# A two-layer graph network on one core: projections by seven half-size products, and layer 1's ELU spread over more steps

## The chip, the cores and the metric

The kernel runs on one core of one Trainium2 chip. Its time is the device time of one execution in microseconds (us), and the median of the runs counts. The engines are TensorE (PE), VectorE (DVE), ScalarE (ACT), GpSimd (POOL) and SyncE (SP, which issues most DMAs). Each runs its own instructions in the order in which the program lists them, and waits on semaphores for the others. Everything of weight is in float32; only the masks and the small logit products of layer 1 are bfloat16.

## The reference

There are 4096 nodes with 512 features, and a 4096 x 4096 weighted adjacency matrix `adj`. Each of the two layers normalizes its input, applies relu, runs an attention and adds the result to its input.

```python
h = relu(layernorm(x))                       # layer 0
q, k, v = h @ Wq.T + bq, h @ Wk.T + bk, h @ Wv.T + bv
x = x + softmax(q @ k.T / sqrt(512) + 2 * adj) @ v
h = relu(layernorm(x))                       # layer 1: 8 heads of 64
nX = a_ln * standardized(h @ W, per head) + b_ln
kg = leaky_relu(at1[:, None] + at2[None, :], 0.2) * adj      # per head
y = softmax(where(adj != 0, kg, -32768)) @ nX + nX
x = x + elu(y)
```

## The kernel before

**Projections** (in `fast_path`, lines 545 to 701). The 4096 rows are taken in 8 blocks of 512. `normalize` (L558) takes means and variances of a block (bn_stats, L180), an inverse root (L167 to L172, the power on POOL) and scales the rows on DVE (L564). `hidden` (L569) transposes the block on PE, applies relu on ACT (L575) into `hT`, and forms four sums of quarter blocks, `hS`, on POOL (L583 to L586), both of which are stored for attention. `values_of` (L591) makes 4 tiles of v, each with four matmuls of 512 columns (L595) and one addition of the bias on DVE (L599). `queries` (L604) makes 4 tiles of q against the matrix A, which is Wq and Wk multiplied ahead (L669), in the same way (L609, L613), and forms four sums on POOL (L626 to L629). Four PSUM tiles (tag mm) hold results. The order is that of the program: in round sb it is `normalize` of block sb + 1, `load_x` of block sb + 2, `values_of(sb)`, `hidden(sb + 1)`, the small work on layer 1's weights (`center_weights` L236, `weigh_weights` L242), `queries(sb)`. Ahead of the rounds stands a prologue: loads of x, Wv, Wq and Wk, `turn_blocks` of Wq and Wk on DVE (L485), `values_of(0)`, `attention_vectors` (L200), A, `hidden(1)` and `queries(0)`.

**Attention of layer 0** runs over 8 chunks of 512 rows and 32 tiles of columns. Its scores are made by seven half-size products in place of eight (L740): a 2 x 2 block product in Winograd's form of Strassen's scheme, with sums of the operands formed ahead and results added on DVE (L748). The change does not touch it.

**Layer 1** runs 512 steps: 8 chunks of 512 rows, 2 groups of 4 heads, 32 column tiles. In step n the program issues `values(n - 4)` (PE, L1025), `exponent(n - 3)` (ACT, L1012, 2048 elements), `leaky(n)` (DVE: two operations L996, one product with adj L1001, one addition L1002), `weigh(n)` (POOL, L1009: the product with adj), `z_sums(n + 1)` (PE, L970 and L978, into three PSUM tiles with tag d) and `relu(n + 1)` (ACT, L986). POOL multiplies three heads and DVE one; in a "light" step DVE multiplies two and POOL two. Light are steps 11, 17, 23 and 29 of every 32 (L909). `load_adj` (L912) loads masks (z, nb, nx) and weights (g) for four steps at a time on SP.

When the 32 steps of a group are over, `finish` (L1030) hangs its work on the steps that follow, through a table of offsets d. "mid" is behind the exponent on ACT, "end" behind relu. It copies the sums out of PSUM (L1041), turns them into rows (`to_rows`, PE, L1047), divides (`divide`, DVE, L1056 and L1057), adds own features with a DMA that accumulates (`add`, issued on POOL, L1063), computes ELU in pieces on ACT (`minus` L1072, `exps` L1076, `positive` L1079, `less_one` L1082), adds the two halves and the residual with two more such DMAs, and stores (`close`, SP, L1087). As step n of the table is the fourth step of the next group, offset d falls into step d + 3 of that group.

Of the kernel before, what the change touches and what calls it, by code (L numbers as in the profile page):

```python
# [78 lines left out]
def fast_path(  # L79
# [161 lines left out]

    def weigh_weights(k):  # L242
        for e in range(2):
            t = prep.tile([P, NH, HD], F32, name="prod", tag="prod", bufs=2)
            seq(nc.gpsimd.tensor_mul(t, w1_sb[:, k], aa[e]))
            seq(nc.vector.tensor_reduce(w1a_sb[:, k, e, :], t, AX.X, ALU.add))
# [221 lines left out]
    with tc.tile_pool(name="early", bufs=2) as early, tc.tile_pool(name="kv", bufs=1) as kv:  # L468
# [70 lines left out]
        with tc.tile_pool(name="proj_c", bufs=1) as pc, tc.tile_pool(  # L539
# [10 lines left out]
            bv_sb = early.tile([P, D], F32, name="bv_sb", tag="qt", bufs=16)  # L550
# [7 lines left out]
            def normalize(xt):  # L558
                mv = means(work, [xt[:, b, :] for b in range(SB)], "h")
                var = work.tile([P, SB], F32, name="hv", tag="hv", bufs=1)  # L560
                seq(nc.vector.tensor_scalar_add(var, mv[:, :, 1], LN_EPS))
                rstd = inverse_root(nc.vector, work, var, SB, "h")
                for b in range(SB):
                    seq(nc.vector.tensor_scalar(  # L564
                        xt[:, b, :], xt[:, b, :], mv[:, b, 0:1], rstd[:, b : b + 1],
                        ALU.subtract, ALU.mult,
                    ))
# [22 lines left out]

            def values_of(sb):  # L591
                for b in range(SB):
                    pv = psum.tile([P, 512], F32, name="pv", tag="mm", bufs=4)
                    for k in range(KC):
                        seq(nc.tensor.matmul(  # L595
                            pv, hidden_of[sb][0][:, k, ts(b, P)], wv_sb[k],
                            start=k == 0, stop=k == KC - 1,
                        ))
                    seq(nc.vector.tensor_add(v[:, sb * SB + b, :], pv, bv_sb))  # L599
# [3 lines left out]

            def queries(sb):  # L604
                qs = pc.tile([P, KC, GC], F32, name="qs", tag="qs", bufs=1)
                for o in range(KC):
                    pq = psum.tile([P, 512], F32, name="pq", tag="mm", bufs=4)
                    for k in range(KC):
                        seq(nc.tensor.matmul(  # L609
                            pq, a_sb[:, k, ts(o, P)], hidden_of[sb][0][:, k, :],  # L610
                            start=k == 0, stop=k == KC - 1,
                        ))
                    seq(nc.vector.tensor_scalar(  # L613
                        sources_of_rows(qs[:, o, :]), pq.rearrange("p (c q r) -> p c q r", c=SB, r=R),
                        c_sb[:, o : o + 1], half_scale, ALU.add, ALU.mult,
                    ))
# [36 lines left out]
            normalize(xts[0])  # L653
# [3 lines left out]
            for name in ("q", "k"):  # L657
                for c in range(SB):
                    turn_blocks(turned[name][:, c, :], raw[name], c)
            values_of(0)  # L660
            normalize(xts[1])
# [4 lines left out]
            for k in range(KC):  # L666
                pa_ps = psum.tile([P, 512], F32, name="pa", tag="mm", bufs=4)
                for c in range(SB):
                    seq(nc.tensor.matmul(  # L669
                        pa_ps, turned["q"][:, c, ts(k, P)], turned["k"][:, c, :],  # L670
                        start=c == 0, stop=c == SB - 1,
                    ))
                seq(nc.scalar.copy(a_sb[:, k, :], pa_ps))
            seq(nc.vector.tensor_reduce(c_sb, wk_rows, AX.X, ALU.add))
            xts[2] = load_x(2)
            hidden(1, xts[1])
            queries(0)
            for sb in range(1, NS):
                if sb + 1 < NS:
                    normalize(xts[sb + 1])  # L680
# [14 lines left out]
                if sb + 1 < NS:  # L695
                    hidden(sb + 1, xts[sb + 1])
                if sb == 2:
                    center_weights()
                elif 3 <= sb < 3 + KC:
                    weigh_weights(sb - 3)  # L700
                queries(sb)
# [195 lines left out]
    with tc.tile_pool(name="ga_in", bufs=2) as inputs, tc.tile_pool(  # L897
# [11 lines left out]
        light = {n for n in range(n_steps) if n % NB in (11, 17, 23, 29)}  # L909
# [120 lines left out]
        def finish(n, ic, hg):  # L1030
# [47 lines left out]
            def positive():  # L1078
                seq(nc.scalar.activation(flat(y), flat(y), AF.Relu))  # L1079

            def less_one():
                seq(nc.scalar.add(flat(grp["e"]), flat(grp["e"]), -1.0))  # L1082
# [8 lines left out]
            for d, place, f in (  # L1091
                (0, "mid", copies),
                (1, "mid", lambda: to_rows(0)), (1, "end", lambda: divide(0)),
                (2, "mid", lambda: to_rows(1)), (2, "end", lambda: divide(1)),
                (3, "end", lambda: add(y, of_group(own_d))),
                (6, "end", room), (6, "end", lambda: minus(0)), (7, "end", lambda: minus(1)),
                (8, "end", lambda: exps(0)), (8, "end", positive), (9, "end", lambda: exps(1)),
                (10, "end", less_one), (11, "end", lambda: add(grp["e"], flat(y))),
                (14, "end", lambda: add(grp["e"], of_group(x1_d))), (17, "end", close),
# [36 lines left out]
        for n in range(n_steps + 22):  # L1136
# [458 lines left out]
```

## Time and profile before

| what | value |
|---|---|
| median of 3 runs | 3947.59 us (3941.22 to 3955.6) |
| profiled execution, its own time | 3945.4 us |
| its span, first to last instruction | 3943.6 us |
| projections, 0 to 271 us | PE busy 254.6 us |
| attention of layer 0, 271 to 2090 us | PE busy 1782.3 us |
| first group of layer 1, 2090 to 2254.5 us | POOL busy 127.3 us, DVE 119.5 us |
| other fifteen groups, 2254.5 to 3905 us | POOL busy 1629.4 us, DVE 1574.0 us, ACT 1420.3 us |
| tail, 3905 to 3943.6 us | ACT busy 10.4 us |

A row of the profile names the engine, the line of the kernel, the operation and the tiles that it writes and reads. An engine's busy time is the time in which one of its instructions runs; the ends of matmuls are modelled, so the distance between starts says more than the duration. One float32 matmul leaves two records. Clock is the share of TensorE's full clock that was granted.

### The profile page before, as it was taken

Reading aid. Unit: us, or ns where it says so; the run is one execution under the profiler, and the core shown is the slowest. Engines: PE = TensorE matmul, PEld = TensorE weight load, DVE = VectorE, ACT = ScalarE, POOL = GpSimd, SP = SyncE. Lnnn points to the kernel's source line nnn. Section 1 sums busy time; section 2 is a strip of 40 time slices with the busy share of each in tenths; the row PEclk is TensorE's granted clock in tenths of the full one; section 3 lists DMA queues with packets and bytes.
Section 4 is the critical chain, followed back from the end, with each engine's and each line's share of the span. In section 5 each row is a group of like instructions: output and inputs, shape, how many; then the busy total and the mean of one; then the engine's idle time right before and its main releaser. Section 6 shows DMA issues by size and latency. Waiting matters only on the chain. (4 is left out here: it accounts for less than half of the span.)

```text
span 3943.6 us, 48614 instructions
## 1 busy us (share of the span) xinstructions
PE 3697.2 (94%) x17418; PEld 1722.2 (44%) x17418; DVE 2869.3 (73%) x4299; ACT 1779.9 (45%) x1581; POOL 2501.3 (63%) x1321
## 2 busy tenths in 40 slices
PE   8989999999999999999997889999999999999996
PEld 4446666666666666666663222222222222222221
DVE  5435556565465656556566799999999999999996
ACT  1001011111111111111114688888888888888886
POOL 3432225243252524324256899999999999999996
PEclk9999999999999999999998899999999999999998
DMA  6466766768585676767567777676676777766774
GB/s 206 178 200 192 207 179 198 210 183 225 164 216 173 199 207 190 216 176 214 164 176 190 188 188 190 184 186 183 191 191 188 189 188 196 188 185 182 189 192 107
DMA packets 622778, 746.17 MB, mean 189 GB/s; under 512 B 84672, under 2 KB 467904, under 8 KB 603072
## 3 DMA queue, kind: packets, MB, share of 16 engines
q1 hardware_dynamic: 613552, 716.05, 64.3%
q0 software_dynamic: 6912, 25.17, 3.6%
q8 instruction: 138, 2.26, 0.2%
q10 hardware_dynamic: 2064, 1.77, 0.2%
q14 instruction: 112, 0.92, 0.1%
HBM read 562.23 MB, written 172.23 MB: 186 GB/s over the span
## 5 line engine op out<-in xcount | busy, mean ns | idle before, releaser
L1009 POOL TENSOR_TENSOR t<-t,g 128x1536 f32<-128x1536 f32 (+1 forms) x512 | 1704.8, 3531 | 55.7 <-DVE t L1002 48.1
L1025 PE MATMUL acc<-t,nX 128*64 128x512 f32 x4096 | 1001.7, 610 | 49.4 <-ACT t L1012 44.3
L758 POOL TENSOR_TENSOR total<-total,aT 128x512 f32<-128x512 f32 x248 | 340.1, 1371 | 1064.0 <-ACT aT L753 1055.2
L1012 ACT ACTIVATE t<-t 128x2048 f32<-128x2048 f32 x512 | 974.9, 1905 | 1.5 <-POOL t L1009 1.5
L768 PE MATMUL acc<-v,aT 128*128 128x512 f32 x2048 | 963.0, 593 | 0.0
L753 ACT ACTIVATE aT<-aT 128x512 f32<-128x512 f32 x256 | 161.2, 630 | 1323.7 <-DVE aT L748 1301.6
L986 ACT ACTIVATE t<-d 128x1024 f32<-128x1024 f32 x512 | 524.5, 1024 | 285.0 <-PE d L978 284.8
L1002 DVE TENSOR_TENSOR t<-t,d 128x1024 f32<-128x1024 f32 x512 | 619.2, 1209 | 2.8 <-ACT t L986 2.8
L768 PEld LDWEIGHTS acc<-v,aT 128*128 128x128 f32 x2048 | 390.0, 190 | 273.7 <-issue 245.6
L1025 PEld LDWEIGHTS acc<-t,nX 128*64 128x64 f32 x4096 | 251.5, 137 | 564.5 <-issue 344.7
L970 PE MATMUL d<-z,z 6*128 6x512 bf16 x2048 | 370.9, 387 | 108.2 <-DVE t L1001 59.4
L996 DVE SCALAR_TENSOR_TENSOR d<-u,at2m,d 128x512 f32<-128x512 f32 x576 | 431.7, 749 | 39.2 <-PE d L978 34.9
L748 DVE TENSOR_TENSOR aT<-aT,X 128x256 f32<-128x256 f32 x512 | 214.6, 419 | 290.0 <-PE X L740 287.0
L1001 DVE TENSOR_TENSOR t<-d,g 128x512 f32<-128x512 f32 (+1 forms) x512 | 383.9, 750 | 14.4 <-DMA g<-gT_d 7.8
L748 DVE TENSOR_TENSOR aT<-aT,Z 128x256 f32<-128x256 f32 x384 | 159.4, 415 | 306.5 <-PE Z L740 301.8
L996 DVE SCALAR_TENSOR_TENSOR t<-u,at2m,d 128x512 f32<-128x512 f32 x448 | 334.5, 747 | 46.5 <-DVE d L996 1.4
L970 PEld LDWEIGHTS <-z 6*128 6x128 bf16 x2048 | 91.9, 91 | 624.5 <-issue 404.3
L978 PE MATMUL d<-nx,ident_b 64*64 64x512 bf16 x2048 | 321.2, 392 | 1.4 <-DMA nx<-nT_d 1.2
L978 PE MATMUL d<-nb,ident_b 64*64 64x512 bf16 x2048 | 320.7, 392 | 0.0
L732 DVE SCALAR_TENSOR_TENSOR gs<-ng,aT 128x512 f32<-128x512 bf16 x256 | 279.4, 1091 | 10.2 <-DMA gT_d<-gs 1.5
L740 PE MATMUL Z<-qt,hS 128*128 128x256 f32 x1024 | 265.7, 382 | 8.3 <-DVE aT L748 8.3
L740 PE MATMUL X<-qt,hT 128*128 128x256 f32 x1024 | 264.3, 381 | 0.5 <-DVE aT L748 0.5
(171 smaller groups left out, 3154.2 us busy)
## 6 DMA issues: line engine op xcount, KB each, us to landing
g<-gT_d SPq DMA_DIRECT2D x128, 1024.0 KB, 5.5
ag<-in_adj_dram SPq DMA_DIRECT2D x256, 256.0 KB, 5.7
hT<-h_d SPq DMA_DIRECT2D x64, 1024.0 KB, 6.0
hS<-s_d SPq DMA_DIRECT2D x64, 1024.0 KB, 8.2
gT_d<-gs SPq DMA_DIRECT2D x256, 256.0 KB, 2.8
nb<-nT_d SPq DMA_DIRECT2D x128, 512.0 KB, 4.7
nx<-nT_d SPq DMA_DIRECT2D x256, 256.0 KB, 5.6
nT_d<-ng SPq DMA_DIRECT2D x256, 128.0 KB, 3.2
```

Of the source, the lines that this page charges most:

```text
L740: seq(nc.tensor.matmul(out, a, b, start=start and k == 0, stop=k == 1, skip_group_check=not start,))
L748: seq(nc.vector.tensor_add(p, p, part))
L768: seq(nc.tensor.matmul(sums[ic][b], probs[s][:, ts(b, P)], v[:, jt, :], start=jt == 0, stop=jt == NB - 1))
L970: seq(nc.tensor.matmul(pair[hh // 2][:, hh % 2, :], z2[rows, ts(jt % JB, P)], groups[ic, hg]["z1"][rows, :], start=True, stop=False,))
L978: seq(nc.tensor.matmul(pair[hh // 2][ts(c, HD), hh % 2, :], ident_b[rows, rows], masks[r != c][rows, jt % JB, :], start=False, stop=True,))
L986: seq(nc.scalar.activation(t[:, 0:2, :], zs[n][0], AF.Relu, scale=4.0))
L996: seq(nc.vector.scalar_tensor_tensor(pair[1][:, e, :] if e > 1 - mine else t[:, 2, :], u4[:, e, :], at2m[:, jt, h : h + 1], pair[1][:, e, ...
L1001: seq(nc.vector.tensor_mul(t[:, HG - mine : HG, :], pair[1][:, 2 - mine : 2, :], g))
L1002: seq(nc.vector.tensor_add(t[:, 0:2, :], t[:, 0:2, :], pair[0]))
L1009: seq(nc.gpsimd.tensor_mul(t[:, 0:mine, :], t[:, 0:mine, :], g))
L1012: seq(nc.scalar.activation(logits[n], logits[n], AF.Exp))
L1025: seq(nc.tensor.matmul(grp["acc"][hf][ts(e, HD), :], nX[jt // SB][:, jt % SB, hg * HG + 2 * hf + e, :], t[:, 2 * hf + e, :], start=jt == 0 ...
```

## The change

It has two independent halves.

In the projections, `values_of` and `queries` use seven half-size products each, for two lanes at a time (a lane is a pair of row tiles, or one of two output tiles). Each product is two matmuls of 256 columns; each result is taken out of PSUM by DVE into a half tile, as it stands or on top of what is there. PSUM holds two X and two Z tiles in place of four of 512 columns. The second operands' sums are formed on POOL (`sum_wv`, `sum_a`); the first operands' sums are those that `hidden` makes already. The factor 0.5 / sqrt(512) moves into A and its bias. Means stay on DVE, the rest of the normalization goes to POOL and ACT, and it is done a round earlier; `center_weights` and `weigh_weights` stand behind `queries`, and the weights' sums a round later.

In layer 1, three steps of 32 are light, at 8, 23 and 26. The divisions stand 3 steps apart, `positive` and `less_one` work on halves, and ELU's eight pieces on ACT lie at offsets 7 to 19 in place of 6 to 10. The accumulating DMAs are at 5, 20 and 23 in place of 3, 11 and 14, the store at 26 in place of 17.

```diff
+    def sum_weighed(k):
+        for e in range(2):
+            seq(nc.vector.tensor_reduce(w1a_sb[:, k, e, :], weighed.pop((k, e)), AX.X, ALU.add))
...
+            wv_sums, a_sums = [
+                [early.tile([P, KC // 2, H], F32, name=name, tag="qt", bufs=16) for _ in range(4)]
+                for name in ("wvs", "as")
+            ]
...
-            def normalize(xt):
+            def deviations_of(xt):
                 mv = means(work, [xt[:, b, :] for b in range(SB)], "h")
                 var = work.tile([P, SB], F32, name="hv", tag="hv", bufs=1)
-                seq(nc.vector.tensor_scalar_add(var, mv[:, :, 1], LN_EPS))
-                rstd = inverse_root(nc.vector, work, var, SB, "h")
+                seq(nc.gpsimd.tensor_scalar_add(var, mv[:, :, 1], LN_EPS))
+                rstd = inverse_root(nc.gpsimd, work, var, SB, "h")
+                shift = work.tile([P, SB], F32, name="hs", tag="hs", bufs=2)
+                seq(nc.gpsimd.tensor_mul(shift, mv[:, :, 0], rstd))
+                seq(nc.gpsimd.tensor_scalar_mul(shift, shift, -1.0))
+                return rstd, shift
+
+            def normalize(xt, rstd, shift):
                 for b in range(SB):
-                    seq(nc.vector.tensor_scalar(
-                        xt[:, b, :], xt[:, b, :], mv[:, b, 0:1], rstd[:, b : b + 1],
-                        ALU.subtract, ALU.mult,
+                    seq(nc.scalar.activation(
+                        xt[:, b, :], xt[:, b, :], AF.Identity,
+                        scale=rstd[:, b : b + 1], bias=shift[:, b : b + 1],
                     ))
...
+            def seven(product, take):
+
+                x, z = [
+                    [psum.tile([P, H], F32, name=name, tag=name, bufs=2) for _ in range(2)]
+                    for name in ("X", "Z")
+                ]
+                for n, todo in enumerate((
+                    ((2, z, "11", True), (1, x, "11", False)), ((5, z, "22", True), (6, x, "12", True)),
+                    ((3, z, "12", False), (7, x, "22", False)), ((4, x, "21", True),),
+                )):
+                    for lane in range(2):
+                        for which, t, _, _ in todo:
+                            product(lane, which, t[lane], which in (1, 2, 5))
+                        for _, t, block, first in todo:
+                            take(lane, block, t[lane], first)
+
+            def pair_product(out, a, b, start):
+                for k in range(2):
+                    seq(nc.tensor.matmul(
+                        out, a[k], b[k], start=start and k == 0, stop=k == 1,
+                        skip_group_check=not start,
+                    ))
...
             def values_of(sb):
+                def product(pair, which, out, start):
+                    a, b = SIDES[which]
+                    pair_product(out, side_a(sb, pair, a), wv_side(b), start)
+
+                def take(pair, block, part, first):
+                    half = ts(int(block[1]) - 1, H)
+                    to = v[:, sb * SB + 2 * pair + int(block[0]) - 1, half]
+                    seq(nc.vector.tensor_add(to, part, bv_sb[:, half] if first else to))
+
+                seven(product, take)
...
             load_blocks(raw["k"], wkT)
             xts[1] = load_x(1)
             seq(nc.sync.dma_start(out=wk_rows, in_=wkT.rearrange("(k p) o -> p k o", p=P)))
-            normalize(xts[0])
+            of_next = deviations_of(xts[0])
+            sum_wv()
+            normalize(xts[0], *of_next)
             hidden(0, xts.pop(0))
...
+            of_next = deviations_of(xts[1])
             values_of(0)
-            normalize(xts[1])
+            normalize(xts[1], *of_next)
             attention_vectors(v[:, 15, :])
...
-                pa_ps = psum.tile([P, 512], F32, name="pa", tag="mm", bufs=4)
+                pa_ps = psum.tile([P, 512], F32, name="pa", tag="mm", bufs=2)
...
-                seq(nc.scalar.copy(a_sb[:, k, :], pa_ps))
+                seq(nc.scalar.mul(a_sb[:, k, :], pa_ps, half_scale))
             seq(nc.vector.tensor_reduce(c_sb, wk_rows, AX.X, ALU.add))
+            seq(nc.vector.tensor_scalar_mul(c_sb, c_sb, half_scale))
+            sum_a()
             xts[2] = load_x(2)
             hidden(1, xts[1])
+            of_next = deviations_of(xts[2])
             queries(0)
+            normalize(xts[2], *of_next)
             for sb in range(1, NS):
-                if sb + 1 < NS:
-                    normalize(xts[sb + 1])
...
                 values_of(sb)
                 if sb + 1 < NS:
                     hidden(sb + 1, xts[sb + 1])
+                if sb + 2 < NS:
+                    of_next = deviations_of(xts[sb + 2])
+                if 4 <= sb < 4 + KC:
+                    sum_weighed(sb - 4)
+                queries(sb)
                 if sb == 2:
                     center_weights()
-                elif 3 <= sb < 3 + KC:
+                if 3 <= sb < 3 + KC:
                     weigh_weights(sb - 3)
-                queries(sb)
+                if sb + 2 < NS:
+                    normalize(xts[sb + 2], *of_next)
...
-        light = {n for n in range(n_steps) if n % NB in (11, 17, 23, 29)}
+        light = {n for n in range(n_steps) if n % NB in (8, 23, 26)}
...
-                (2, "mid", lambda: to_rows(1)), (2, "end", lambda: divide(1)),
-                (3, "end", lambda: add(y, of_group(own_d))),
-                (6, "end", room), (6, "end", lambda: minus(0)), (7, "end", lambda: minus(1)),
-                (8, "end", lambda: exps(0)), (8, "end", positive), (9, "end", lambda: exps(1)),
-                (10, "end", less_one), (11, "end", lambda: add(grp["e"], flat(y))),
-                (14, "end", lambda: add(grp["e"], of_group(x1_d))), (17, "end", close),
+                (4, "mid", lambda: to_rows(1)), (4, "end", lambda: divide(1)),
+                (5, "end", lambda: add(y, of_group(own_d))),
+                (7, "end", room), (7, "end", lambda: minus(0)), (9, "end", lambda: minus(1)),
+                (10, "end", lambda: exps(0)), (12, "end", lambda: exps(1)),
+                (14, "end", lambda: positive(0)), (15, "end", lambda: positive(1)),
+                (17, "end", lambda: less_one(0)), (19, "end", lambda: less_one(1)),
+                (20, "end", lambda: add(grp["e"], flat(y))),
+                (23, "end", lambda: add(grp["e"], of_group(x1_d))), (26, "end", close),
...
-        for n in range(n_steps + 22):
+        for n in range(n_steps + 31):
```

## The prediction

> **What bounds the kernel now.** I read the page first, then the table of windows by stage.
>
> ```profile
> PE 3697.2 (94%) x17418; PEld 1722.2 (44%) x17418; DVE 2869.3 (73%) x4299; ACT 1779.9 (45%) x1581; POOL 2501.3 (63%) x1321
> 49.80:271.00 221.20, 218.29 (x578) 101.06 (x576) 97.83 (x191) 13.82 (x26) 88.81 (x71) 1.00 0.55 190
> 2254.50:3905.00 1650.50, 1520.33 (x9822) 419.04 (x9822) 1573.96 (x1978) 1420.33 (x1080) 1629.37 (x533) 1.00 0.70 186
> ```
>
> The page's shares mix three stages. In the windows (columns PE, PEld, DVE, ACT, POOL busy, clock, DMA share, GB/s) the projections, up to 271 us, are PE's: 218.29 of 221.20 us. Attention of layer 0 (271 to 2090) the change does not touch. In layer 1, 2254.5 to 3905, POOL is busy 99% and DVE 95%, so the chain of waits decides which of them sets the step.
>
> Projections, PE's timeline (start, duration, count), then the same from attention, where half-size products already run:
>
> ```profile
> 93.42 13.90 PE L595 MATMUL pv<-wv_sb,hT 128*128 128x512 f32 x32
> 107.15 1.04 PE L574 MATMUL pt<-ident,xt 128*128 128x128 f32 x8
> 109.55 13.90 PE L609 MATMUL pq<-hT,a_sb 128*128 128x512 f32 x32
> 123.29 7.89 PE L595 MATMUL pv<-wv_sb,hT 128*128 128x512 f32 x18
> ...
> 999.77 1.03 PE L740 MATMUL Z<-qt,hS 128*128 128x256 f32 x4
> 1000.63 1.03 PE L740 MATMUL X<-qt,hS 128*128 128x256 f32 x4
> ```
>
> Only starts count, since ends are modelled. 32 records of 512 columns take 123.29 - 109.55 = 13.74 us, 0.429 each; 4 of 256 columns take 1000.63 - 999.77 = 0.86, 0.215 each. Each written matmul leaves two records.
>
> Layer 1, the chain of waits in order of time (start, us, what) within one group of 32 steps:
>
> ```profile
> 3267.26 1.13 DVE t L1002
> 3271.42 1.13 DVE t L1002
> 3274.67 1.13 DVE t L1002
> ...
> 3342.61 1.13 DVE t L1002
> 3345.86 1.13 DVE t L1002
> 3349.78 1.12 DVE t L1002
> 3353.02 1.14 DVE t L1002
> ```
>
> and POOL's timeline of the same group:
>
> ```profile
> 3244.80 27.50 POOL L1009 TENSOR_TENSOR t<-t,g 128x1536 f32<-128x1536 f32 x8 [0.63 <-DVE t L1002]
> 3276.04 0.89 POOL L1063 DMA_DIRECT2D y<-own_d  x1
> 3276.66 26.67 POOL L1009 TENSOR_TENSOR t<-t,g 128x1536 f32<-128x1536 f32 x8
> ```
>
> A plain step is 3.25 us on DVE, one with a division 4.16 to 4.20, a light one 3.92: 32 x 3.25 + 4 x 0.66 + 2 x 0.94 = 108.5. The groups from 2920 on measure 109.43 at best, so 0.9 is left; in the starts of L1002 it is two steps of 3.83 and 3.69 where ACT's ELU pieces delay relu. POOL: (27.50 - 3.47) / 7 = 3.43 for three heads; its starts give 2.42 for two heads, and 0.62, 0.62 and 0.91 per adding DMA issued: 28 x 3.43 + 4 x 2.42 + 2.15 = 107.9. So DVE leads by 0.6, with the 0.9 of ACT on top.
>
> **What the Trainium skill says.** "TensorE: Matmul & The Clock Gate", Back-to-back issue gap: spacing is linear in columns; the trace agrees (0.215 against 0.429). The same page, What's actually happening: after about 3.4 us idle the array runs at half clock until a busy window has passed; here a wait of 2.7 us before 31.94 was followed by clock 0.50 from 33.03 to 36.44. "SBUF — State Buffer", Who interferes with whom: a VectorE instruction with two SBUF inputs and a GpSimd one exclude each other for a whole instruction; one 128x4 product (L169) took 4.45 us beside L663's 4.50. "DMA: Bandwidth & Descriptors", Issuing engines are not separate DMA queues: all share 16 engines; e<-x_d, issued just ahead of mask loads, lands in 8.0 us (median), y<-own_d, issued behind them, in 5.6.
>
> **The change, part by part.**
>
> *Half-size products.* A block had 32 records of 0.429 = 13.74; now 7 products x 2 lanes x 2 x 2 = 56 records of 0.215 = 12.03. That is 1.71 less. From 49.8 to 271 there are 8 queries and 7 values: **-25.7**. What hides the rest: DVE adds 14 half blocks of some 0.42 (L748) per call in place of 4 of 0.68 to 0.75, 5.9 us beside 12; normalizing leaves DVE for ACT (4 x 0.6, ACT is 6% busy); its small operations go to POOL, 3.0 us per block as at 2109.20 to 2112.24, beside 10 of sums and 2.5 of weighing in 26 us. A lane's takes have the other lane's 1.7 us of PE. bn_stats (3.2) and weight sums (1.4) queue ahead of the queries' takes, with transposes (2.4) and the first products (3.4) as cover. No price, but nothing spare.
>
> *New sums on POOL.* sum_wv is 8 subtractions of 256 columns, about 0.7 each (half of L583's 1.27), while PE waits for raw k; without that cover up to 5.6. sum_a is 4 of 1.27 after the last copy of A; its first result is due 1.3 later, and transposes and first products give 5.8. hidden(1)'s sums then end some 11 after A, values(1) asks for them 15 later. Nothing.
>
> *Prologue.* Four PSUM tiles used to take all of values(0); now after 3.4 us PE needs DVE's takes, queued behind the turning of raw k (ready at 31.24 today) and bn_stats of x block 1 (3.2). Today PE waits 2.73 and starts the A product at 31.94. Four ACT DMAs move behind a normalize, so k and x may land some 3.5 earlier: takes at 30.8, PE again at 31.2, then 8.6 of products: 39.8, that is **+8** (11.5 if k lands as now, 6 at best). The late DMAs reach attention_vectors about 44; its 10.6 on DVE and c_sb's 2.3 end near 58 to 61, just when the queries need takes.
>
> *center_weights* moves behind queries(2): 2.3 + 0.2 + 3.4 on DVE, the last with two SBUF inputs beside POOL's sums. values(3)'s takes stand behind it for some 7.6 us, where PE has 3.4 of products: 4.2 idle, and 1.7 if the clock halves for 3.4 us: **+5.9** (4 to 8). Before, four PSUM banks hid it.
>
> *Layer 1.* One light step less: DVE -0.66, POOL +1.01. DVE alone 107.9, POOL 29 x 3.43 + 3 x 2.42 + 2.15 = 108.9. So POOL becomes the bound, and of the 1.6 that DVE sheds only 0.55 is left. Halved ELU pieces: each 0.6 puts ACT 0.3 behind (exp 1.9 + relu 1.0 of a step's 3.25), and relu ends 1.2 before DVE needs it (3283.2 against 3284.4 in step 10), so spread pieces fit; today's, 1.05 long among neighbours, go past that. Their cover gone, the 0.9 would be back on DVE, still within POOL's queue. Divisions apart: same two at 0.94.
>
> *y's load* is issued after step 8 (a light one) and minus(0) follows 2 steps on, where it had 3. Behind minus(0) on ACT stand exp(8) and relu(12), for which DVE waits. From the start of L1002 in step 8: issue at 1.2 + 2.4 + 0.1 + POOL's lag, then the landing, then 0.5 + 1.8 + 1.0 on ACT, against 4 x 3.25 = 13.0: DVE stalls by lag + landing - 5.9. POOL meanwhile has 2.42 + 0.62 + 3 x 3.43 = 13.3 of work and its lag, so it idles only past a landing of 6.2. The load meets the second half of g's 1 MB; I put it at 6.2 to 6.5: +0.3 a group. Fifteen groups: 15 x (108.9 + 0.3) + 4 x 2.7 (own products of the last chunk, L368 and L369) = 1648.8 against 1650.4 now, **-1.6**. The tail has 8 ACT pieces of 0.62 for 4.6 us today: +0.4. On SP, close waits for e<-x_d as today, between two quads' loads: nothing. The two adding DMAs into e stay 3 steps apart (10 us; the first lands in 4.7 to 7.0). The longer loop adds no work.
>
> Sum: -25.7 + 8 + 5.9 - 1.6 + 0.4 = -13. The profiled execution took 3945.4 (span 3943.6), the runs' median 3947.6. 3945.4 - 13 = **3932**.
>
> **Rivals.**
> - *y lands late* (slower). If it takes 8.2, as e<-x_d does, POOL idles 2.0 a group instead of 0.3: 15 x 1.7 = 26; at 8.5, 30: 3932 + 30 = 3962. It decides from a landing of 7.4 (13 / 15 beyond 6.5). For it: g is still moving. Against: the mask loads come 3.5 us later.
> - *The projections' stalls eat their gain*: k lands as now, the clock halves more than once, takes come late in every block: 3.5 + 1.7 + 14 x 0.5 = 12, 3944. For it: DVE's order leaves nothing spare. Against: x lands 12.1 us after a block's values start (75.66 against 63.53), as their takes end.
> - *Half-size products save nothing* because a take is late at every lane: 3932 + 26 = 3958. Against: attention keeps PE at 98% (1782 of 1819 us) on such pairs.
> - *POOL does not bind*, its lag being absorbed: 107.9 a group, 20 less: 3912. Against: POOL's own sum.
>
> **How the numbers follow.** Chances: forecast 0.50 (own range 3922 to 3942), late y 0.20, stalls 0.14, no saving 0.07, no bind 0.09. About 0.3% is 11.8 us, what a measurement can tell: bounds 3935.8 and 3959.4. Of the forecast two thirds lie below 3935.8, and all of the last: 0.41. Late y above 3959 about 0.14, no saving 0.04, and 0.07 for a halved clock that stays: 0.25 slower. The rest 0.34. Range 3914 to 3962.
>
> **What would show it.** Right: 12.0 us from the first record of a values block to the transposes; PE idle near 19 to 31 and once near 125; L1002 steps of 109 us a group with POOL never waiting. Wrong: ACT's L1072 waiting for y in every group with POOL idle behind it, groups above 110, or gaps between lanes.

## The result, and the profile after

The changed kernel took 3939.1 us (median of 12 runs, 3931.84 to 3943.88), the kernel before beside it 3942.05 us (median of 12). The ratio of the runs is 0.9986, 95% interval 0.9979 to 0.9994: about 5 us less, where 13 were forecast (the two medians lie 3 us apart). The profiled execution took 3934.7 us, its span is 3933.0, against 3943.6 before.

The busy times, first part of the page of the changed kernel:

```profile
PE 3666.0 (93%) x17802; PEld 1794.8 (46%) x17802; DVE 2879.1 (73%) x4388; ACT 1803.6 (46%) x1645; POOL 2536.5 (64%) x1389
```

PE is busy 31 us less and POOL 35 us more. Where the time went is seen only by stage, from the starts of the same instructions in both traces:

| stretch | before, us | after, us | difference | forecast |
|---|---|---|---|---|
| start to the first product of queries(0) | 49.80 | 56.01 | +6.2 | +8 |
| from there to attention's first product | 221.46 | 201.15 | -20.3 | -25.7 + 5.9 |
| attention of layer 0 | 1822.0 | 1817.1 | -4.9 | 0 |
| to the first addition (L1002, now L1107) of group 1 | 161.3 | 160.4 | -0.9 | 0 |
| groups 1 to 15 of layer 1 | 1650.4 | 1658.0 | +7.6 | -1.6 |
| tail | 38.7 | 40.2 | +1.5 | +0.4 |

The change doesn't touch attention: over the traces of all kernels in this document it takes 1817 to 1826 us. So 5 us of this pair's 10.6 are taken as no effect of the change. The first row varies too: in the ten traces with this prologue queries(0) begins at 54.4 to 58.6 us.

The windows of the changed kernel (columns as before: PE, PEld, DVE, ACT, POOL busy, clock, DMA share, GB/s):

```profile
16.60:39.95 23.35, 15.30 (x57) 12.45 (x57) 13.48 (x29) 3.53 (x5) 12.03 (x13) 0.78 0.92 268
56.01:257.10 201.09, 195.51 (x938) 170.49 (x936) 117.69 (x261) 31.41 (x50) 99.59 (x116) 0.99 0.61 209
2234.70:3892.80 1658.10, 1515.65 (x9822) 419.31 (x9822) 1564.18 (x1978) 1420.16 (x1110) 1641.23 (x533) 0.99 0.68 185
```

In the prologue PE is busy for 15.3 of 23.35 us at clock 0.78. In the projections proper it works without a gap of more than 0.6 us but for one. In layer 1 POOL has 11.9 us more to do than before and still stands idle for 17 us.

PE's timeline (start, duration, in brackets the idle time before and what ended it):

```profile
19.75 1.03 PE L625 MATMUL X<-wv_sb,hT 128*128 128x256 f32 x4
28.72 2.05 PE L625 MATMUL Z<-wvs,hS 128*128 128x256 f32 x4 [7.95 <-POOL hv L571]
...
68.10 1.03 PE L625 MATMUL Z<-wv_sb,hT 128*128 128x256 f32 x4
...
80.18 1.04 PE L590 MATMUL pt<-ident,xt 128*128 128x128 f32 x8
...
123.57 1.03 PE L625 MATMUL X<-wv_sb,hT 128*128 128x256 f32 x4
128.15 1.10 PE L625 MATMUL Z<-wvs,hS 128*128 128x256 f32 x4 [3.55 <-DVE v L660]
129.09 1.59 PE L625 MATMUL X<-wvs,hS 128*128 128x256 f32 x4
```

A block of values now takes 80.18 - 68.10 = 12.08 us. Twice PE waits: 7.95 us in the prologue (the row names POOL, which had long been done; what ends the wait is DVE's first take at 28.18) and 3.55 us in values(3). After both waits its records are stretched (1.59 to 2.05 us in place of 1.03), because TensorE was then granted half its clock.

In layer 1 the fifteen groups divide in two. Groups 5 to 14 take 109.19 us on average (109.80 before). Groups 1 to 4 take 113.09, 117.21, 114.83 and 113.84 (before 112.72, 111.04, 110.58, 110.64). ACT's timeline of group 2, from the trace after:

```profile
2392.90 0.63 ACT L1177 ACTIVATE e<-y 128x512 f32<-128x512 f32 x1 [7.81 <-DMA y<-own_d]
2393.44 1.89 ACT L1117 ACTIVATE t<-t 128x2048 f32<-128x2048 f32 x1
2395.24 1.00 ACT L1091 ACTIVATE t<-d 128x1024 f32<-128x1024 f32 x1
```

minus(0) waits 7.81 us for y, and exp(8) and relu(12) stand behind it. POOL's timeline beside it:

```profile
2383.69 0.82 POOL L1168 DMA_DIRECT2D y<-own_d  x1
2384.31 10.44 POOL L1114 TENSOR_TENSOR t<-t,g 128x1536 f32<-128x1536 f32 x3
2397.57 3.44 POOL L1114 TENSOR_TENSOR t<-t,g 128x1536 f32<-128x1536 f32 x1 [2.82 <-DVE t L1107]
2403.31 10.34 POOL L1114 TENSOR_TENSOR t<-t,g 128x1536 f32<-128x1536 f32 x3 [2.30 <-DVE t L1107]
```

The load of y is issued at 2383.69 and lands at 2392.88; POOL has three weighings left, then runs dry, twice. The waits of that group (who waited for whom: us in all, times, the longest):

```profile
ACT e L1177 <- DMA y<-own_d: 7.8, 1, 7.8
...
DVE t L1107 <- ACT t L1091: 6.8, 1, 6.8
POOL t L1114 <- DVE t L1107: 5.1, 2, 2.8
```

In group 9 the first of these rows reads 1.0 us and the last is missing: POOL's queue covers it. Over the fifteen groups ACT waits 34.2 us for y; in the kernel before it was 1.6.

A second stall follows the first. PE waits for exp(8), which stands behind minus(0), and then works at half clock:

```profile
2395.38 3.68 PE L1130 MATMUL acc<-t,nX 128*64 128x512 f32 x8 [8.20 <-ACT t L1117]
```

These are the products values(8), in 3.68 us, where eight such records took 1.94 at 2383.86; the clock is 0.50 from 2395.3 to 2399.0. z_sums(13) comes behind them on PE, so DVE waits for it, 2.4 us in this group. Over the fifteen groups the second stall costs DVE as much as the first:

```profile
DVE t L1107 <- ACT t L1091: 19.8, 10, 6.8
DVE d L1101 <- PE d L1083: 19.3, 15, 2.7
```

The second stall is 1.9 to 2.7 us in groups 1 to 4, 7 and 10, where half clock fell on it, and 0.5 in the nine others. Six kernels below leave minus(0) where the change puts it. Counted with them, the step from 12 took 4.9 to 6.1 us in the 45 groups in which half clock fell on it, and at most 3.9 in the other 60. In the kernel before no such step exists; there groups 5 and 8, at 110.9 us, are the ones in which half clock fell on a step with ELU pieces (5.5 and 5.2 us for the step from 13, in place of 3.8).

### The profile page after: what moved, and what is told of

Read it like the earlier page. It is cut to its first block, busy times and chain, and to the rows that moved or that the text cites. A ratio compares the mean times of both kernels' runs of the same rounds, so it can differ in the third digit from the quotient of the medians.

```text
span 3933.0 us, 49742 instructions
## 1 busy us (share of the span) xinstructions
PE 3666.0 (93%) x17802; PEld 1794.8 (46%) x17802; DVE 2879.1 (73%) x4388; ACT 1803.6 (46%) x1645; POOL 2536.5 (64%) x1389
## 5 line engine op out<-in xcount | busy, mean ns | idle before, releaser
L1114 POOL TENSOR_TENSOR t<-t,g 128x1536 f32<-128x1536 f32 (+1 forms) x512 | 1722.7, 3680 | 49.2 <-DVE t L1107 40.9
L1107 DVE TENSOR_TENSOR t<-t,d 128x1024 f32<-128x1024 f32 x512 | 619.3, 1210 | 22.8 <-ACT t L1091 22.6
L1101 DVE SCALAR_TENSOR_TENSOR d<-u,at2m,d 128x512 f32<-128x512 f32 x560 | 419.4, 749 | 42.7 <-PE d L1083 40.2
L1075 PE MATMUL d<-z,z 6*128 6x512 bf16 x2048 | 358.4, 388 | 91.4 <-DVE t L1106 44.7
L1101 DVE SCALAR_TENSOR_TENSOR t<-u,at2m,d 128x512 f32<-128x512 f32 x464 | 346.5, 747 | 48.1 <-DVE d L1101 1.8
L1106 DVE TENSOR_TENSOR t<-d,g 128x512 f32<-128x512 f32 (+1 forms) x512 | 375.2, 733 | 6.0 <-DMA g<-gT_d 0.9
```

Of the source, the lines that this page charges most:

```text
L1075: seq(nc.tensor.matmul(pair[hh // 2][:, hh % 2, :], z2[rows, ts(jt % JB, P)], groups[ic, hg]["z1"][rows, :], start=True, stop=False,))
L1101: seq(nc.vector.scalar_tensor_tensor(pair[1][:, e, :] if e > 1 - mine else t[:, 2, :], u4[:, e, :], at2m[:, jt, h : h + 1], pair[1][:, e, ...
L1106: seq(nc.vector.tensor_mul(t[:, HG - mine : HG, :], pair[1][:, 2 - mine : 2, :], g))
L1107: seq(nc.vector.tensor_add(t[:, 0:2, :], t[:, 0:2, :], pair[0]))
L1114: seq(nc.gpsimd.tensor_mul(t[:, 0:mine, :], t[:, 0:mine, :], g))
```

## The experiments

The theory after these readings: the projections give what was forecast, some 14 us less; layer 1 loses about 8, because y lands too late for minus(0) in four groups (no run separates the half clock behind it from the wait itself). Rivals: the gain was never in the projections but in attention's own spread; or layer 1 loses by POOL's load alone, or by the light steps.

All are compared with runs of the kernel before on the same chip. The groups' times, each from one profiled execution:

| kernel | ratio to before (95%) | groups 1-4, mean | 5-14, mean | sum 1-15 |
|---|---|---|---|---|
| before | 1 | 111.25 | 109.80 | 1650.4 |
| changed | 0.9986 (0.9979-0.9994) | 114.74 | 109.19 | 1658.0 |
| own 13 steps later | 0.9980 (0.9973-0.9986) | 111.94 | 109.67 | 1650.9 |
| minus(0) 1 step later | 0.9961 (0.9947-0.9974) | 112.05 | 108.70 | 1641.3 |
| ELU 2 steps later | 0.9947 (0.9933-0.9961) | 110.37 | 109.05 | 1638.6 |
| ELU 2 later, four light | 0.9927 (0.9914-0.9941) | 109.55 | 108.51 | 1629.7 |
| own on DVE | 1.0014 (1.0008-1.0021) | 116.51 | 109.16 | 1664.4 |
| four light | 1.0037 (1.0023-1.0051) | 115.27 | 110.19 | 1672.1 |

### Each half alone

The first kernel has the changed projections and layer 1 as before; the second has layer 1 as changed and the projections as before. The diff is the change's own, one half of it each.

> The projections as changed, layer 1 as before. Theory (the half-size products pay 25.7 us, prologue and center_weights give some of it back; layer 1's half loses in the first groups): attention's first product near 257 us as in the changed kernel (271 before), groups of layer 1 at 109.4 as before, in all 14 to 16 us faster than before, ratio 0.996. Rival (the projections' gain is lost again further on, and layer 1's half is what gained): ratio 0.999 to 1.000.

> Layer 1 as changed, the projections as before. Theory: groups 5 to 15 about 0.6 us shorter each (108.5 to 109.5 where nothing disturbs), groups 1 to 4 some 3.5 us longer each (113 to 117), in all 7 to 11 us slower than before, ratio 1.002 to 1.003. Rival (POOL's sum is the only thing that counts): every group shorter or equal, ratio 0.998 to 0.999.

Measured: 3928.5 us, ratio 0.9961 (0.9947 to 0.9974), that is 15 us less, for the projections; 3953.27 us, ratio 1.0028 (1.0016 to 1.0040), 11 us more, for layer 1. Together -4, and both at once gave -5: the halves add. Attention starts at 256.4 in the first and 272.15 in the second (271.26 before), and groups 1 to 4 of the second average 113.95. So the gain comes from the projections and the loss from layer 1's half.

### The own products 13 steps later

```diff
-                at_step(36 + 32 * b, own, b)
+                at_step(49 + 32 * b, own, b)
```

> The changed kernel, with the last chunk's own products (two POOL operations, 2.7 us) 13 steps later, in step 18 of groups 1 to 4 in place of step 5. Theory (they put POOL behind just ahead of the issue of y's load, so y lands late, ACT waits and POOL then runs dry): ACT's longest wait for y falls from 7.8 to below 2 us, groups 1 to 4 fall from 113 to 117 to about 111.5 (108.8 and the 2.7), 11 to 13 us less than the changed kernel, ratio 0.995 to 0.996. Rival (those groups are long because POOL has 2.7 us more to do and the mask loads are slow there): groups 1 to 4 stay above 113, ratio as the changed kernel's 0.9986.

Measured: 3935.76 us, ratio 0.9980 (0.9973 to 0.9986): a miss, a few us at most in place of the expected gain, and the interval overlaps the changed kernel's. The trace tells why. POOL is the bound, so it is slow to work off own's 2.7 us: from group 3 on, part of the lag that own leaves in step 18 is still there in step 8 of the next group. POOL's lag at step 8 is now 0.1, 0.1, 1.2, 1.9 and 2.3 us in groups 1 to 5 (2.5, 3.8, 3.2, 3.0 and 0.1 in the changed kernel), and the groups take 112.1, 110.0, 112.2, 113.5 and 113.5 us. Group 5, which had been free of it, now pays too. In groups 1 and 2, where y is in time, DVE waits 3.2 and 1.1 us in step 28 for a load of the weights g. The experiment moved the cause and didn't take it away.

### minus(0) one step later

```diff
-                (7, "end", room), (7, "end", lambda: minus(0)), (9, "end", lambda: minus(1)),
+                (7, "end", room), (8, "end", lambda: minus(0)), (9, "end", lambda: minus(1)),
```

> The changed kernel, with ELU's first piece at offset 8 in place of 7, so that y's load has a step more. Theory: ACT no longer waits for y in groups 5 to 15 (they come to 108.5 to 108.9 without the 110 and 111 among them), and groups 1 to 4 lose 3 us of the wait, to about 111.5 to 113; 9 to 14 us less than the changed kernel, ratio 0.995 to 0.9965. Rival (the piece, once it stands next to its neighbours at 9 and 10, puts ACT behind again): the gain is under 4 us.

Measured: 3927.87 us, ratio 0.9961 (0.9947 to 0.9974), 10 us less than the changed kernel's 0.9986. In groups 5 to 14 POOL no longer waits at all. From one step 8 to the next it takes 108.96 us, which is the 108.9 of the prediction's sum; DVE's groups take 108.70, since POOL falls 2.4 us behind over the ten groups. In groups 2, 3 and 4 y lands in 9.75, 7.25 and 8.24 us and ACT still waits 6.1, 1.8 and 3.8.

### ELU two steps later, then with four light steps

The first kernel moves all from `room` to `close`, the second also changes the light steps:

```diff
-                (7, "end", room), (7, "end", lambda: minus(0)), (9, "end", lambda: minus(1)),
...
+                (9, "end", room), (9, "end", lambda: minus(0)), (11, "end", lambda: minus(1)),
...
-        light = {n for n in range(n_steps) if n % NB in (8, 23, 26)}
+        light = {n for n in range(n_steps) if n % NB in (8, 14, 20, 26)}
```

> The changed kernel with all of ELU's work, from the room for it and minus(0) to the store, two steps later (offsets 9 to 28 in place of 7 to 26); the load of y stays where it is. Theory (y lands too late for minus(0), in groups 1 to 4 by much, in the others by about 1 us): y has 6.5 us more, so no wait for y is left anywhere. POOL then is the bound of every group: 28 weighings of 3.43, 3 of 2.42 and so on, 108.75 a group, and 2.7 more in groups 1 to 4 for the own products. Fifteen groups 15 x 108.75 + 10.8 = 1642, where the changed kernel measured 1658: 16 us less, a ratio to the kernel before of about 0.9945 to 0.9955. Rival (the one step that the other run gave y is all there is; what is left in groups 1 to 4 is the own products' own time): no more than with minus(0) alone one step later, 0.996.

> As the run before it, with four light steps in place of three (8, 14, 20, 26 of every 32). Theory (once y is no longer waited for, POOL is the bound with three light steps by about 1 us a group, and the own products' 2.7 us fit into what POOL then has spare): POOL has 107.9 of work a group and DVE 108.5, fifteen groups of about 108.6 = 1630, 28 us less than the changed kernel; ratio to the kernel before 0.992 to 0.9935. Rival (DVE's own time binds all along): each light step costs its 0.66 in every group, so 10 us more than the run before it.

Measured: 3925.43 us, ratio 0.9947 (0.9933 to 0.9961), and 3915.06 us, ratio 0.9927 (0.9914 to 0.9941). The fifteen groups take 1638.6 (expected 1642) and 1629.7 (expected 1630). With ELU later, ACT's wait for y is left in one group alone (2.0 us in group 2). With four light steps besides, the windows of the second read:

```profile
2240.71:3870.40 1629.69, 1519.34 (x9820) 421.54 (x9822) 1571.21 (x1978) 1418.14 (x1110) 1624.35 (x533) 1.00 0.69 188
```

POOL has 17 us less work than in the changed kernel, DVE 7 more, and most groups take 108.43: that is, within 0.1 us, DVE's 32 steps of 3.25, 0.66 more for each of four light ones and 0.94 more for each of two divisions, and nothing else. The rival, that DVE bound all along, falls: four light steps cost nothing here, they gave 9 us.

### Four light steps alone

The same line of light steps, ELU as in the change.

> The changed kernel with four light steps (8, 14, 20, 26) in place of three, ELU where the change puts it. Theory (y's landing decides in groups 1 to 4, and DVE has nothing spare with four light steps, so its waits behind minus(0) count in full): groups 1 to 4 at about 113, groups 5 to 14 at 108.5 + 0.4 to 0.6, the fifteen groups 1648, 10 us less than the changed kernel, ratio to the kernel before 0.996. Rival (the number of light steps alone gave the gain of the run that had both): 1630, 28 us less, 0.992.

Measured: 3959.52 us, ratio 1.0037 (1.0023 to 1.0051): slower than the changed kernel, where 10 us less had been expected. The rival is out, since the light steps alone gave no gain; but the size that the theory gave was wrong as well. In the changed kernel a late y costs DVE two steps in every group: with three light steps in groups 5 to 14 the step from 11 takes 3.24 to 4.25 us and that from 12 mostly 3.89, in place of 3.25, and POOL's queue covers nearly all of it. With four light steps there is no such cover. From the waits of group 9, where POOL did not wait in the changed kernel:

```profile
POOL t L1114 <- DVE t L1107: 1.7, 3, 0.9
```

In groups 5 to 14 the step from 11 is 0.60 us longer than 3.25 on average and that from 12 1.06 (three of the ten met half clock). 108.5 + 1.7 = 110.2, which is their mean (110.19). The second of the two late steps is what the formula of the prediction left out.

### The own products on DVE

```diff
-            seq(nc.gpsimd.tensor_mul(o, features(b), over_heads(aln_sb)))
-            seq(nc.gpsimd.tensor_add(o, o, over_heads(bln2_sb)))
+            engine = nc.vector if last else nc.gpsimd
+            seq(engine.tensor_mul(o, features(b), over_heads(aln_sb)))
+            seq(engine.tensor_add(o, o, over_heads(bln2_sb)))
```

> The changed kernel with the two operations of own (a product and a sum of 128x512 in step 5 of groups 1 to 4, 1.36 and 1.28 us on POOL) on DVE, where a product of that size takes 0.69 us (L210); nothing else is moved. Theory (own puts POOL behind, so that the load of y is issued 2.7 us later and meets the mask loads, and minus(0), relu and exp wait): the same work on DVE leaves POOL's lag at step 8 at 0.1 us as in groups 5 to 14, y lands in 6 to 6.5 us, and groups 1 to 4 take DVE's 107.9 + 1.4 + 0.4 to 1.2, that is 109.7 to 110.5 in place of 114.75: 17 to 20 us less than the changed kernel, a ratio to the kernel before of 0.9935 to 0.9945. Rival (y lands late in groups 1 to 4 for another reason, such as own's stores or the other work of these groups): landings of 7 to 9 us stay, groups of 112 or more, at most 11 us less, a ratio of 0.996 or above.

Measured: 3951.59 us, ratio 1.0014 (1.0008 to 1.0021): a miss in time. On y the theory held all the same. Its load is issued 3.6 to 3.7 us after step 8 begins in the groups read; in the changed kernel that is 6.06, 7.33, 6.70 and 6.53 us in groups 1 to 4 and 3.6 in the others. The mask loads z, nb and nx are issued at 7.1 to 8.7 us. y lands in 5.67, 5.64, 5.53 and 6.38 us in groups 1 to 4 (5.92, 9.19, 7.02 and 6.61 in the changed kernel), and ACT waits 0.6, 0.5, 0.4 and 1.3 (3.3, 7.8, 5.0 and 4.4). The time is lost elsewhere, between the additions of steps 4 and 5. The timeline of DVE and POOL there, in group 1:

```profile
2256.30 6.89 POOL L1115 TENSOR_TENSOR t<-t,g 128x1536 f32<-128x1536 f32 x2
2258.90 4.83 DVE L374 TENSOR_TENSOR own<-x,aln_sb 128x512 f32<-128x512 f32 x1
2263.77 0.69 DVE L375 TENSOR_TENSOR own<-own,bln_sb 128x512 f32<-128x512 f32 x1
2267.78 6.95 POOL L1115 TENSOR_TENSOR t<-t,g 128x1536 f32<-128x1536 f32 x2 [4.60 <-DVE t L1108]
```

The product has two SBUF inputs and ends only after POOL's running weighing and the one queued behind it are done, at 2263.19: 4.83 us in place of 0.69. POOL then idles 4.60. That stretch takes 9.7 to 11.0 us in place of 4.2. That a VectorE instruction with two SBUF inputs and a GpSimd one that reads SBUF exclude each other for a whole instruction is what the Trainium skill says ("SBUF — State Buffer", Who interferes with whom). This trace agrees, and the expectation should have priced it. So the run shows that own's lag makes y late, and doesn't measure what own's work is worth without it.

### The subtraction of center_weights in four pieces

```diff
-        seq(nc.vector.tensor_sub(w1_sb, w1_sb, m.unsqueeze(3).to_broadcast([P, KC, NH, HD])))
+        middle.append(m)
+
+    middle = []
+
+    def center_piece(k):
+        seq(nc.vector.tensor_sub(
+            w1_sb[:, k], w1_sb[:, k], middle[0][:, k, :].unsqueeze(2).to_broadcast([P, NH, HD])
+        ))
...
+                    center_piece(sb - 3)
                     weigh_weights(sb - 3)
```

> The changed kernel with the subtraction of center_weights (one DVE instruction of 3.4 us over 2048 columns) cut into four of 512 columns, each ahead of its weigh_weights in rounds 3 to 6; layer 1 as in the changed kernel. Theory (values(3)'s takes stand behind that one instruction, PE waits 3.55 us and then runs at half clock): the wait and the half clock go, the block values(3) takes 12.1 in place of 17.6 us, the first product of attention starts at about 252 in place of 257.2, the time is 5 us less, a ratio to the changed kernel of 0.9987 and to the kernel before of about 0.9973. Rival (the wait comes from the order of all three instructions of center_weights or from POOL's sums): a wait of 2 us or more stays at 124, and the gain is below 2 us.

Measured: 3935.2 us, ratio 0.9974 (0.9963 to 0.9984), as expected. As this interval overlaps the changed kernel's, the trace has to carry the reading. PE's timeline at the same place:

```profile
124.05 1.03 PE L632 MATMUL X<-wv_sb,hT 128*128 128x256 f32 x4
125.28 1.10 PE L632 MATMUL Z<-wvs,hS 128*128 128x256 f32 x4 [0.21 <-DVE v L667]
126.22 1.03 PE L632 MATMUL X<-wvs,hS 128*128 128x256 f32 x4
```

The wait is 0.21 in place of 3.55, the clock stays full, values(3) takes 12.5 us in place of 17.6, and attention starts at 252.6 in place of 257.16.

### The means of x block 1 behind values_of(0)

```diff
-            of_next = deviations_of(xts[1])
             values_of(0)
+            of_next = deviations_of(xts[1])
             normalize(xts[1], *of_next)
```

> The changed kernel with one line of the prologue moved: the means and variances of x block 1 (bn_stats, 3.2 us on DVE, waiting for x until 25.6) behind values_of(0) in place of ahead of it. Theory (PE's wait from 20.6 to 28.7 ends with the first take, which stands behind bn_stats): the takes start when raw k is turned, at about 24.5; PE waits 4 us in place of 7.95, queries(0) and all that follows start about 3.7 us earlier; first product of attention at 253.5, 3.7 us less than the changed kernel, ratio to it 0.999. The half clock after the wait stays, since 2.7 us of waiting brought it on in the kernel before. Rival (what comes later on DVE, attention_vectors and c_sb, then holds up queries(0)): queries(0) starts at 56 as now, no gain.

Measured: 3946.3 us, ratio 1.0005 (0.9999 to 1.0012), 7 us more than the changed kernel by the ratios. The rival held, and more than held. PE's timeline:

```profile
24.28 1.10 PE L625 MATMUL Z<-wvs,hS 128*128 128x256 f32 x4 [2.46 <-DVE v L660]
...
43.47 8.73 PE L765 MATMUL pa<-v 128*128 128x512 f32 x16 [3.45 <-ACT a_sb L769]
...
61.72 2.05 PE L625 MATMUL Z<-hS,as 128*128 128x256 f32 x4 [3.74 <-DVE qs L705]
```

and ACT's:

```profile
40.01 0.81 ACT L580 ACTIVATE xt<-xt,hs,hr 128x512 f32<-128x512 f32 x1 [22.34 <-POOL hs L575]
40.26 0.33 ACTq L202 DMA_DIRECT2D a_sb<-in_a1T_dram  x1
```

The wait of 7.95 us shrinks to 2.46 and A begins at 32.99 in place of 39.95. But `normalize` of block 1 on ACT now begins at 40.01 in place of 31.47, and ACT keeps its order. The copies of A out of PSUM stand behind it, so PE waits 3.45 for a tile; the DMAs for attention_vectors stand in it, so that part of DVE's work ends later, c_sb and the next means with it, and the first take of queries(0) comes at 61.12 in place of 57.08. Attention starts at 263.3 in place of 257.2. The 7 us saved became two waits of 3.5 and 3.7 us, each with half clock after it, and in values(3) the half clock lasted 6.9 us where it was 3.4.

### All together, and one step too far

The first kernel joins ELU two steps later, four light steps and the four pieces. The second moves ELU one more step (offsets 10 to 29) and has the means behind values_of(0).

> Both together: ELU two steps later, four light steps, and the subtraction in four pieces. The two lie in different stages, so the gains should add: 28 + 5 = 33 us less than the changed kernel, a ratio to the kernel before of 0.990 to 0.992. If the gain of one depends on the other, the sum falls short.

> The best so far (ELU two steps later, four light steps, the subtraction in four pieces) with ELU one more step later (offsets 10 to 29) and the means of x block 1 behind values_of(0). In the run before it ACT still waited 2.95 and 1.68 us for y in groups 2 and 4, which cost these groups 3.8 and 1.5 us; one step more takes these waits away, and the prologue gives 3.7: 8 to 9 us less than that run, ratio to the kernel before about 0.9885 to 0.989. Rival (the stores of y that wait in turn, or the room for e that comes free later, then hold up the loads of the next group): no gain from the step, 3.7 at most.

Measured: 3909.96 us, ratio 0.9908 (0.9894 to 0.9921), for the first: the gains add, 31 us less than the changed kernel by the ratios, and it is the fastest of all. The second took 3929.15 us, ratio 0.9964 (0.9952 to 0.9976): a miss. ACT waits for y in no group, as the theory said, and that is worth nothing, because another wait replaces it: `room` takes the buffer of `ob`, so the copies of the next group's sums wait for the store of this one. From group 7's timeline:

```profile
2913.29 1.07 ACT L1154 COPY ob<-acc 128x512 f32<-128x512 f32 x2 [1.73 <-DMA out_dram<-e]
2914.02 3.42 PE L1138 MATMUL acc<-t,nX 128*64 128x512 f32 x8 [2.18 <-ACT ob L1154]
2915.32 1.22 DVE L1115 TENSOR_TENSOR t<-t,d 128x1024 f32<-128x1024 f32 x1 [1.24 <-ACT t L1099]
```

In this group the steps from 3 and 4 take 4.56 and 6.37 us in place of 3.25 and 4.20, and groups 5 to 14 average 109.63 (108.53 in the first kernel). The fifteen groups take 1643.5 us (1631.0 in the first kernel). The prologue's move adds 4 us until attention, where it added 6 to the changed kernel. The rival, a store that holds up the next group, is the one that the trace shows.

## Why the prediction was right and where it was wrong

The time lies in the range and a small gain was forecast, but the sum as it stands did not come out: its first three terms came near, the fourth had the wrong sign. That the total still fell inside is owed to the width of the range (3914 to 3962), since layer 1 was 9.2 us off where 13 were forecast.

**Half-size products, -25.7.** A block takes 12.08 where 12.03 was worked out. From queries(0) to attention the difference is -20.3; without the 5.5 of center_weights that is -25.8. Right, and "nothing spare" on DVE was enough.

**Prologue, +8.** A begins at 39.95 (39.8 forecast), 8.0 later than before. The place was right: the first take stands behind bn_stats of block 1. That the time agrees so well is luck. PE resumed at 28.72 where 31.2 was put down, and then needed 11.2 us for the products where 8.6 were, since half clock lay on them until 33.8. In other traces with the same prologue A begins at 38.3 to 42.5. The product A itself ran at full clock and took 13.74 in place of 15.54, since its half clock was now spent in values(0). Of the 8 us 6.2 were left. That a remedy cannot simply swap the two is what the prediction had said of the late DMAs; the run with the means behind shows it.

**center_weights, +5.9.** values(3) takes 17.56, 5.5 more than 12.08. The run with four pieces takes away 4.6 of it. Right in place and size.

**Layer 1, -1.6: wrong, +7.6.** For groups 5 to 14 the working held: POOL became the bound, y lands in 6.0 to 7.0 us, ACT waits 0.8 to 1.9 us, and the mean is 109.19 where 109.2 was put down. Groups 1 to 4 took 114.74 where 108.9 + 0.3 + 2.7 = 111.9 was expected: 11 us in four groups. Group 15, counted to its last addition, takes 107.2 where the sum put 109.2, which leaves the 9.2 between +7.6 and -1.6. Two steps of the working failed in groups 1 to 4.

The first is "4 x 2.7 (own products of the last chunk, L368 and L369)". Own's work was counted as POOL's time alone. It stands in step 5, three steps ahead of the issue of y, on the same engine, so POOL's lag at the issue is 2.4 to 3.6 us there. "The mask loads come 3.5 us later" was true without this lag; with it the load is issued 1.0 us ahead of the first mask load in group 1, 0.4 and 0.6 in groups 3 and 4, and behind it in group 2. The landings are 5.92, 9.19, 7.02 and 6.61 us where 6.2 to 6.5 was put down. The formula for the first stall held: "lag + landing - 5.9" gives 2.4, 6.9, 4.1 and 3.5 us, and the step from 11 is longer by 2.4, 6.9, 4.1 and 3.6.

The second is that nothing was put down for what comes behind the first stall. The prediction counts POOL's lag also as POOL's cover, so that POOL "idles only past a landing of 6.2". By that rule the four groups would have cost 0, 3.0, 0.8 and 0.4 us, 4 in all; POOL idled 2.0, 5.1, 3.3 and 2.5, 13 in all. The rest is the second stall: PE runs values(8), which waits for exp(8), ahead of z_sums(13), and in these groups at half clock. DVE waits 2.7, 2.4, 2.7 and 2.4 us there, where 0.5 is usual without half clock. The difference, 8 us in four groups, is an estimate of what the half clock cost; no run takes it away alone.

**The rivals.** "y lands late" decides from a landing of 7.4: that was reached in one group of fifteen (9.19). But the place that it named was right, L1072 (now L1177) waiting for y and POOL idle behind it. "No bind", with 107.9 a group, fell: with three light steps POOL's 108.9 is the floor, as the run with minus(0) one step later shows. "Stalls eat the gain" and "no saving" fell with the first half alone, which gave 15 us.

What stays open: the runs don't separate the mask loads from other traffic as what stretches y's landing. In the changed kernel and its variants the landings above 8.5 us all belong to loads issued among the mask loads. But in group 1 a load issued 1 us ahead of them landed in 5.92, and with ELU two steps later two loads that were issued at the same moment as g's 1 MB, 3 us ahead of the masks, took 8.4.

## What to carry to other kernels

A load that is issued from a compute engine's queue is as late as that queue: before an instruction is hung on its arrival, add the engine's lag at the issue, with all that stands ahead in the queue, in each phase of the program and not only in the steady one. When one engine loses its slack, look for the waits that the slack had covered, and for what a wait does to TensorE's clock behind it. Give consumers of transfers their room first; only then does balancing the engines pay (four light steps alone made the fifteen groups 14 us longer, with ELU later they made them 9 shorter). And before a stalled instruction is moved behind another, list what follows on its consumers' queues, DMAs and buffers' next users too.

## What the runs showed of the hardware

- The accumulating DMA of 512 KB landed in 5.5 to 5.7 us in groups 1 to 3 of the kernel with own on DVE (issued 3.6 us after step 8 began, g's load 3.7 us ahead of it), in 6.0 to 7.0 us in groups 5 to 14 of the changed kernel (issued at the same place, g's load 1.4 to 2.2 us ahead), and in up to 10.16 us among the mask loads (the fastest kernel, group 2, issued 8.18 us after that start).
- A wait of PE doesn't decide by its length alone whether half clock follows. The same wait of 3.55 us ahead of values(3) was followed by it in eight of nine kernels, and not in the one with ELU two steps later and four light steps (129.44, its records stay at 1.03 us). In the kernel before a wait of 1.2 us just ahead of step 13 was followed by it in groups 5 and 8 and not in the thirteen others. 2.73 us in the prologue was enough there, and 2.46 in the kernel with the means behind was not.
- In all fourteen traces a stretch of half clock lasts 3.4 us or a whole multiple of it (3.4, 6.8, 10.2 and so on), but for the one that is open at the end. The Trainium skill ("TensorE: Matmul & The Clock Gate", What's actually happening) gives a free-running window of about 3.4 us, whose place varies by half a microsecond, and half clock after an idle one. The lengths agree with that window; that the array must be idle for the whole of one does not fit the waits of 1.2 to 2.73 us above.
- One DVE product of 128x512 with two SBUF inputs took 4.83 us beside POOL's weighings, one running and one queued, and an operation of the same form 0.69 without.
